# Moving the sums of a step's pairs behind the first bank of the second layer

## The chip, the cores and the metric

The kernel runs on one core of one Trainium2 chip. Its time is the device time of an execution in microseconds (us). Times of one kernel are compared through the median of several runs. Engines are named as in the profile: PE is TensorE (the matmuls), PEld its weight loads, DVE is VectorE, ACT is ScalarE, POOL is GpSimd, SP is SyncE, which issues DMA transfers.

## The reference

A layer of a graph network: 6250 nodes with 128 features (`x`), 100,000 edges (`src`, `dst`) sorted by destination, a hidden width of 256.

```python
msg_in = concatenate([x[src], x[dst]], axis=-1)
h = relu(msg_in @ Wm1 + bm1)
h = relu(h @ Wm2 + bm2)
messages = h @ Wm3 + bm3
agg = segment_sum(messages, dst) / clip(count, 1)[:, None]
upd = relu(concatenate([x, agg]) @ Wn1 + bn1) @ Wn2 + bn2
return layernorm(x + (x + upd))
```

All inputs and the output are 32-bit floats (indices are integers).

## The kernel before

**Tables.** A prelude of some 85 us multiplies `x` by the two halves of `Wm1`: `atab` holds the half for the source, in 32-bit floats, `btab` the half for the destination, split into bf16 terms. Both lie in DRAM. `Wm3` is linear and is applied to a node's mean, behind the segment sum.

**Steps.** The edges come in 196 groups of 512 and the main loop runs over 98 steps of two groups. Iteration p works on several steps at once, in this order in the text of the program (lines of the kernel before):

- `turned` (L770): TensorE turns the partial sums of step p-3, six transposes into two banks, and DVE adds them to the windows of `acc` (`pair_window`, L743; `add_up`, L779, from step 82 on). Called T below.
- `node_steps(p, 0)`: pieces of the node network for finished nodes, in some steps.
- `make_hot(p + 1)`: DVE makes the one-hot matrices of the next step (L640, L642).
- `first_layer` of step p: 32 transposes of the gathered rows (L666), 16 for each group (X0, X1), then the products of btab's rows with the one-hot matrices (L674, four for each group; L683, eight for each group, from step 59 = `B_PAIRED` on; P0, P1). Both add into the PSUM tile `ph`. Two relus on ACT (L692) write `h1`.
- `fetch` of step p+1: eight gathers of atab's rows on POOL (L607), four or eight loads of btab's rows issued by SP (L620), which wait for the last product that reads their buffer.
- `summed(p - 2)`: matmuls with one-hot weights that add up the messages of a destination, 16 instructions in tiles 128*32 (`pair_sums`, L734, up to step 81 = `PAIRED` - 1; `sums`, L724, behind). Called S. ACT copies the result to `part` (`part_of`, L752).
- `second_layer` of step p-1: h1 times Wm2 in four banks of eight matmul instructions (L711), A and B for group 0, C and D for group 1; after each bank DVE takes the maximum with a row that stands for relu and bias, into `h2s` (L714). Between B and C stands `node_steps(p, 1)`, whose matmuls are those of L811, L817 and L844.

**What sets the order.** The order on each engine is the program's own: TensorE, ACT, POOL, SP and DVE run under `tc.manual_schedule`, which keeps the instructions of an engine in the order in which they are written. Semaphores are put in from the buffers that are read and written.

**Buffers.** PSUM has four banks that go round (`bank`): T takes two, S one, A to D one each, so a plain step with paired sums takes seven, in the order T0 T1 S A B C D. `h2s` has one copy for each group: the sums read what the four maxima of the iteration before wrote, and the maxima of this iteration wait until the sums have read. `h1`, `part` and the gathered rows have two copies.

**Marks.** A gather keeps TensorE's pace by three waits (`MARKS`): the first gather of a fetch for a step's sums (`("sums", 0)`), the fifth for the first matmul of bank D (`("second", 12)`), the seventh for the first product (`("products", 0)`).

```python
MARKS = {("sums", 0): 0, ("second", 12): 4, ("products", 0): 6}
```

**Matmuls of 32-bit floats** in banks and sums are two instruction pairs each (a weight load and a matmul), which the profile counts one by one.

Of the kernel before, what the change touches and what calls it, by code (L numbers as in the profile page):

```python
# [14 lines left out]
ALU = mybir.AluOpType  # L15
# [5 lines left out]
P = 128  # L21
# [9 lines left out]
def kernel(  # L31
# [36 lines left out]
    nc = tc.nc  # L68
    N, D = x.shape
    E = src.shape[0]  # L70
    H = wm1.shape[1]
    HC = H // P
# [112 lines left out]
    with tc.tile_pool(name="prep", bufs=1) as prep, tc.tile_pool(  # L185
# [249 lines left out]
        def whole(steps):  # L435
            for _ in steps:
                pass
# [105 lines left out]
    with edge, tc.tile_pool(name="wk", bufs=2) as wk, tc.tile_pool(  # L543
# [28 lines left out]
        def follows(key, made):  # L572

            if not straight[0]:
                return
            for old in earlier.get(key, []):
                tc.declare_no_dep(made.ins, old.ins, reason="TensorE's work between the two waits for the first, "
                                  "and the second waits for that work")

        def keep(key, made):  # L580
            if straight[0]:
                earlier[key] = (earlier.get(key, []) + [made])[-4:]
# [7 lines left out]
        def pace(i, stage, n, matmul):  # L590
            if (stage, n) in MARKS:
                paces.setdefault(i, {})[MARKS[stage, n]] = matmul
# [65 lines left out]


        def first_layer(got, ohts, nts, step):  # L660
            for i, ((ag, _, _), nt) in enumerate(zip(got, nts)):
                for c in range(HC):
                    for j in range(GT):
                        for h in range(nt // 2):
                            half = slice(h * HP, (h + 1) * HP)
                            nc.tensor.matmul(ph[:, i, h, c, j * HP:(j + 1) * HP], ag[half, j, c * P:(c + 1) * P],  # L666
                                             ident[half, half], is_transpose=True, start=(c == 0 and j == 0),
                                             stop=False, skip_group_check=True)
            for i, ((_, bw, paired), nt) in enumerate(zip(got, nts)):
                for c in range(HC):  # L670
                    if paired:
                        for h in range(2):
                            half = slice(h * HP, (h + 1) * HP)
                            matmul = nc.tensor.matmul(ph[:, i, h, c, :], bw[half, 0, c * P:(c + 1) * P],  # L674
                                                      ohts[half, i, :], start=False, stop=True,
                                                      skip_group_check=True)
                            pace(step + 1, "products", (i * HC + c) * 2 + h, matmul)
                            last_product[step] = matmul
                        continue
                    for k in range(2):  # L680
                        for h in range(nt // 2):
                            half = slice(h * HP, (h + 1) * HP)
                            matmul = nc.tensor.matmul(ph[:, i, h, c, k * P:(k + 1) * P],  # L683
                                                      bw[half, k, c * P:(c + 1) * P],
                                                      ohts[half, i, k * P:(k + 1) * P], start=False, stop=True,
                                                      skip_group_check=True)
                            if k == 0:
                                pace(step + 1, "products", (i * HC + c) * 2 + h, matmul)
                            last_product[step] = matmul
            h1 = next_h1()  # L690
            if nts == [GT, GT]:
                made = [nc.scalar.activation(h1[:, :, c, :].rearrange("p i (h e) -> p i h e", h=2),  # L692
                                             ph[:, :, :, c, :], AF.Relu, bias=b1[:, c:c + 1]) for c in range(HC)]
                for one in made:
                    follows(("h1", step % 2), one)
                for one in made:
                    keep(("h1", step % 2), one)
                return h1
            for i in reversed(range(len(nts))):
                nh = nts[i] // 2  # L700
                for c in range(HC):
                    nc.scalar.activation(h1[:, i, c, :nh * 2 * P].rearrange("p (h e) -> p h e", h=nh),
                                         ph[:, i, :nh, c, :], AF.Relu, bias=b1[:, c:c + 1])
            return h1

        def second_layer(h1, h2, nt, step, before):
            for j0 in range(0, nt, 2):
                ph2 = bank()
                for j in range(j0, j0 + 2):
                    for c in range(HC):  # L710
                        matmul = nc.tensor.matmul(ph2[:, j - j0, :], h1[:, c, j * P:(j + 1) * P],  # L711
                                                  w2[:, c, :], start=(c == 0), stop=(c == HC - 1))
                        pace(step + 2, "second", before + j * HC + c, matmul)
                made = nc.vector.tensor_tensor(h2[:, j0:j0 + 2, :H], ph2, nb2.to_broadcast([P, 2, H]), op=ALU.max)  # L714
                follows("copied", made)
                keep("largest", made)

        def sums(groups):

# [258 lines left out]
        for i in range(NP + 7):  # L978
            if i == 8:
                late_loads()  # L980

                none = wk.tile([16, (NG * GE - E) // 16 + 1], I32, name="none", bufs=1)
                nc.vector.memset(none, NONE)
                nc.sync.dma_start(dpad[E - 16:].rearrange("(p e) -> p e", p=16), none)
                nc.sync.dma_start(dpad[:E].rearrange("(p e) -> p e", p=16), dst.rearrange("(p e) -> p e", p=16))
            if i < NP:
                c = 2 * i // CG + 1
                if 2 * i % CG == 0 and 1 < c < NG // CG:
                    chunks[c] = chunk(c)
                queues = [(nc.sync, ENG.SP), (nc.scalar, ENG.Activation) if i == 0 else (nc.sync, ENG.SP)]  # L990
                firsts = b_firsts(i, [eng for _, eng in queues])
                st[i] = dict(nts=NTS[2 * i:2 * i + 2])
            p = i - 1
            if p < 0:
                st[i]["got"] = fetch(i, [(srcT[:, 2 * i + k, :], firsts[k]) for k in range(2)], [q for q, _ in queues])
                continue
            if p == 0:
                make_hot(0)
            k = p - 3
            if 0 <= k < NP:  # L1000
                if k < NP - 2:
                    load_firsts(k)
                pt = turned(st[k]["part"], [GT] if k < PAIRED else st[k]["nts"])
                if k < PAIRED:
                    pair_window(pt, st.pop(k)["firsts"])
                else:
                    add_up(pt, st[k]["firsts"], st.pop(k)["nts"])
            node_steps(p, 0)
            if p in X_LATER:
                whole(x_part(X_LATER[p], bank, (nc.scalar, nc.scalar)))  # L1010
            if p + 1 < NP:
                make_hot(p + 1)
            if p == 0:
                clear(3)
            if p < NP:
                s = st[p]
                s["h1"] = first_layer(s.pop("got"), s.pop("ohts"), s["nts"], p)
            if i < NP:
                st[i]["got"] = fetch(i, [(srcT[:, 2 * i + k, :], firsts[k]) for k in range(2)], [q for q, _ in queues],
                                     paces.pop(i, {}))  # L1020
            if p == 0:
                whole(x_part(X_FIRST, bank, (nc.scalar, nc.vector)))
            if 0 <= p - 2 < NP:
                pgs, matmul = summed(p - 2)
                pace(p + 2, "sums", 0, matmul)
                st[p - 2]["part"] = part_of(pgs, [GT] if p - 2 < PAIRED else st[p - 2]["nts"])
            if 0 <= p - 1 < NP:
                s = st[p - 1]
                for j, nt in enumerate(s["nts"]):
                    if p == NP and j == 1:  # L1030
                        load_firsts(NP - 2)
                        load_firsts(NP - 1)
                    second_layer(s["h1"][:, j], h2s[j], nt, p, j * GT * HC)
                    if j == 0:
                        node_steps(p, 1)
            else:
                node_steps(p, 1)
            if p in (1, 2):
                clear(2)
        assert not st and not slots and not plan  # L1040
# [82 lines left out]
```

## Time and profile before

| | us |
|---|---|
| runs: 1331.02, 1341.98, 1339.16; median | 1339.16 |
| the profiled execution | 1348.45 |
| its span, from the first to the last instruction | 1346.7 |
| its granted TensorE clock, share of full speed | 0.976 |

The profile shows one execution. A row of a group reads: line, engine, operation, output<-input, tile, shape, count, then busy us and mean ns of one, then the idle time of the engine just in front of these instructions and what ended most of it. "issue" is a wait that the profile cannot put down to anything. A row of a timeline reads: start, busy us, engine, line, operation, count, and in brackets the idle time before it. A gap of a few tenths of a microsecond between weight loads of different tile shapes is a change of the array's tiling.

The engines that serve TensorE in the groups of the page:

```profile
L607 POOL DMA_INDIRECT rows<-atab,srcT x784 | 746.1, 952 | 485.2 <-issue 166.8
L714 DVE TENSOR_TENSOR h<-bank,nb 128x512 f32<-128x512 f32 x391 | 264.9, 690 | 600.8 <-PE bank L711 407.4
L692 ACT ACTIVATE h<-ph,b 128x1024 f32<-128x1024 f32 x194 | 205.6, 1110 | 789.2 <-remote 393.5
L666 PE MATMUL ph<-ident,rows 64*128 64x64 f32 x3128 | 134.6, 226 | 38.1 <-issue 36.6
```

### The profile page before, as it was taken

Reading aid. Unit: us, or ns where it says so; the run is one execution under the profiler, and the core shown is the slowest. Engines: PE = TensorE matmul, PEld = TensorE weight load, DVE = VectorE, ACT = ScalarE, POOL = GpSimd, SP = SyncE. Lnnn points to the kernel's source line nnn. Section 1 sums busy time; section 2 is a strip of 40 time slices with the busy share of each in tenths; the row PEclk is TensorE's granted clock in tenths of the full one; section 3 lists DMA queues with packets and bytes.
Section 4 is the critical chain, followed back from the end, with each engine's and each line's share of the span. In section 5 each row is a group of like instructions: output and inputs, shape, how many; then the busy total and the mean of one; then the engine's idle time right before and its main releaser. Section 6 shows DMA issues by size and latency. Waiting matters only on the chain.

```text
span 1346.7 us, 26320 instructions
## 1 busy us (share of the span) xinstructions
PE 1237.1 (92%) x10288; PEld 935.8 (69%) x10289; DVE 618.8 (46%) x1502; ACT 335.5 (25%) x500; POOL 793.6 (59%) x854
## 2 busy tenths in 40 slices
PE   8988998999999999999999998989988999999996
PEld 6746666776776667766766766767767677777784
DVE  6754333333333334443444443534445454555675
ACT  4741221122122112222221222221222212223232
POOL 6666665665666666666666665655655655556531
PEclk9999999999999999999999999999999899999998
DMA  7963443433433334334343444434444434344320
GB/s 224 336 207 105 124 116 99 114 106 101 112 108 112 101 107 115 106 108 129 108 110 113 123 114 118 134 111 125 131 115 120 123 111 137 107 118 122 108 58 24
DMA packets 113876, 163.66 MB, mean 122 GB/s; under 512 B 24730, under 2 KB 74592, under 8 KB 113728
## 3 DMA queue, kind: packets, MB, share of 16 engines
q0 software_dynamic: 38160, 103.75, 27.5%
q1 hardware_dynamic: 67292, 44.97, 10.8%
q10 hardware_dynamic: 8292, 13.18, 3.4%
q8 instruction: 82, 1.34, 0.4%
q14 instruction: 50, 0.41, 0.1%
HBM read 142.35 MB, written 19.86 MB: 120 GB/s over the span
## 4 chain that ended last, share of the span: by engine, by line
PE 89%; issue 6%; DVE 4%; DMA 0%; ACT 0%; POOL 0%; DVEq 0%; SPq 0%; ACTq 0%; POOLq 0%
PE bank L711 53%; PE bank L734 11%; PE ph L666 9%; PE bank L770 3%; PE ph L674 2%; PE pbt L315 2%; PE ph L683 2%; PE bank L844 2%; PE bank L811 1%; PE bank L817 1%; PE bank L724 1%; PE pxu L426 1%; DVE h L714 1%; DVE acc L779 0%; DVE span_i L267 0%
## 5 line engine op out<-in xcount | busy, mean ns | idle before, releaser
L607 POOL DMA_INDIRECT rows<-atab,srcT x784 | 746.1, 952 | 485.2 <-issue 166.8
L711 PE MATMUL bank<-w,h 128*128 128x256 f32 x3128 | 722.6, 386 | 8.0 <-DVE h L714 4.1
L711 PEld LDWEIGHTS bank<-w,h 128*128 128x128 f32 x3128 | 592.5, 192 | 139.3 <-issue 52.5
L714 DVE TENSOR_TENSOR h<-bank,nb 128x512 f32<-128x512 f32 x391 | 264.9, 690 | 600.8 <-PE bank L711 407.4
L692 ACT ACTIVATE h<-ph,b 128x1024 f32<-128x1024 f32 x194 | 205.6, 1110 | 789.2 <-remote 393.5
L666 PE MATMUL ph<-ident,rows 64*128 64x64 f32 x3128 | 134.6, 226 | 38.1 <-issue 36.6
L734 PE MATMUL bank<-h,oh 128*32 128x257 f32 x1312 | 155.5, 409 | 12.4 <-issue 1.3
L666 PEld LDWEIGHTS ph<-ident,rows 64*128 64x128 f32 x3128 | 117.2, 141 | 49.7 <-issue 46.5
L734 PEld LDWEIGHTS bank<-h,oh 128*32 128x32 f32 x1312 | 46.8, 112 | 93.8 <-issue 77.1
L743 DVE TENSOR_TENSOR acc<-acc,bank 128x96 f32 x328 | 83.5, 255 | 40.2 <-remote 18.4
L770 PEld LDWEIGHTS bank<-ident,part 64*128 64x128 f32 x681 | 31.1, 137 | 48.1 <-issue 27.6
L770 PE MATMUL bank<-ident,part 64*128 64x64 f32 x681 | 46.8, 237 | 12.6 <-DVE h L714 8.6
L315 PE MATMUL pbt<-w,xT 128*128 128x256 f32 x196 | 47.6, 388 | 5.9 <-DVE rest L340 3.0
L752 ACT COPY part<-bank 128x257 f32<-128x257 f32 x114 | 42.1, 375 | 24.4 <-PE bank L711 17.3
L315 PEld LDWEIGHTS pbt<-w,xT 128*128 128x128 f32 x196 | 36.5, 194 | 13.4 <-DVE rest L340 4.2
L674 PE MATMUL ph<-oht,rows 64*128 64x256 bf16 x472 | 40.1, 275 | 4.2 <-issue 4.2
L683 PE MATMUL ph<-oht,rows 64*128 64x128 bf16 x620 | 32.7, 225 | 10.7 <-issue 10.0
L642 DVE TENSOR_TENSOR oh<-iota_w,dloc 128x256 f32<-128x256 f32 x82 | 34.3, 418 | 0.0
L779 DVE TENSOR_TENSOR acc<-acc,bank 128x63 f32 x126 | 27.8, 221 | 13.3 <-remote 4.5
L683 PEld LDWEIGHTS <-rows 64*128 64x128 bf16 x620 | 23.2, 99 | 14.8 <-issue 14.7
L640 DVE TENSOR_SCALAR oht<-db,iota_p 128x512 bf16<-128x512 bf16 x98 | 31.8, 324 | 0.0
L674 PEld LDWEIGHTS <-rows 64*128 64x128 bf16 x472 | 24.4, 97 | 7.2 <-issue 6.3
(167 smaller groups left out, 613.0 us busy)
## 6 DMA issues: line engine op xcount, KB each, us to landing
rows<-btab SPq DMA_DIRECT2D x544, 32.0 KB
db<-reltab ACTq DMA_DIRECT2D x98, 128.0 KB
rows<-atab,srcT POOLq DMA_INDIRECT x784
btab<-acc SPq DMA_DIRECT2D x24, 384.0 KB
atab<-at SPq DMA_DIRECT2D x24, 256.0 KB
x_sb<-in_x_dram SPq DMA_DIRECT2D x5, 512.0 KB
xd<-in_x_dram SPq DMA_DIRECT2D x6, 256.0 KB
out_dram<-xd SPq DMA_DIRECT2D x6, 256.0 KB
```

The costliest lines, as they stand in the source:

```text
L315: nc.tensor.matmul(pbt[:, a, :], xT[:, (t0 + a) * P:(t0 + a + 1) * P], w1[:, k, :], start=True, stop=True)
L607: gather = nc.gpsimd.indirect_dma_start(out=ag[:, j, :], out_offset=None, in_=atab[:, :], in_offset=bass.IndirectOffsetOnAxis(ap=idx[:, j: ...
L666: nc.tensor.matmul(ph[:, i, h, c, j * HP:(j + 1) * HP], ag[half, j, c * P:(c + 1) * P], ident[half, half], is_transpose=True, start=(c == ...
L674: matmul = nc.tensor.matmul(ph[:, i, h, c, :], bw[half, 0, c * P:(c + 1) * P], ohts[half, i, :], start=False, stop=True, skip_group_check= ...
L683: matmul = nc.tensor.matmul(ph[:, i, h, c, k * P:(k + 1) * P], bw[half, k, c * P:(c + 1) * P], ohts[half, i, k * P:(k + 1) * P], start=Fal ...
L692: made = [nc.scalar.activation(h1[:, :, c, :].rearrange("p i (h e) -> p i h e", h=2), ph[:, :, :, c, :], AF.Relu, bias=b1[:, c:c + 1]) for ...
L711: matmul = nc.tensor.matmul(ph2[:, j - j0, :], h1[:, c, j * P:(j + 1) * P], w2[:, c, :], start=(c == 0), stop=(c == HC - 1))
L714: made = nc.vector.tensor_tensor(h2[:, j0:j0 + 2, :H], ph2, nb2.to_broadcast([P, 2, H]), op=ALU.max)
L734: matmul = nc.tensor.matmul(pg[(2 * i + q) * WN:(2 * i + q + 1) * WN, :H + 1], oh[:, 2 * q + k, :], h2[:, 2 * q + k, :], start=k == 0, sto ...
L743: made = nc.vector.tensor_add(window, window, pts[q // 2][:, 0, :, k:k + WN])
L752: copied.append(nc.scalar.copy(part[:nt * WN, i], pg[:nt * WN, :H + 1]))
L770: nc.tensor.matmul(pts[r][:, i, c, :], rows, ident[half, half], is_transpose=True, start=True, stop=True, skip_group_check=True)
```

## The change

It changes the order of TensorE's instructions in an iteration, and with it that of the others where they follow.

- `first_layer` calls the new `first_group` for one group after the other: X0 P0 X1 P1 in place of X0 X1 P0 P1. The relus follow both, in the new function `relus`.
- `second_layer` is split into `second_bank` (the eight matmuls) and `largest` (DVE's maximum). In an iteration the matmuls of bank A now come in front of the sums; the sums and ACT's copy follow, then the maximum of A, then bank B with its maximum, `node_steps(p, 1)`, and banks C and D as before. The banks go round in the order T0 T1 A S B C D.
- The part of the node network's first layer that iteration 0 makes (`x_part(X_FIRST)`) and the loads of window positions in iteration 98 (`load_firsts`) move by a few instructions.

```diff
         def first_layer(got, ohts, nts, step):
...
+            for i in range(len(nts)):
+                first_group(i, got, ohts, nts, step)
+            return relus(nts, step)
+
+        def first_group(i, got, ohts, nts, step):
+            (ag, bw, paired), nt = got[i], nts[i]
+            for c in range(HC):
+                for j in range(GT):
+                    for h in range(nt // 2):
+                        half = slice(h * HP, (h + 1) * HP)
+                        nc.tensor.matmul(ph[:, i, h, c, j * HP:(j + 1) * HP], ag[half, j, c * P:(c + 1) * P],
+                                         ident[half, half], is_transpose=True, start=(c == 0 and j == 0),
+                                         stop=False, skip_group_check=True)
+            for c in range(HC):
+                if paired:
+                    for h in range(2):
+                        half = slice(h * HP, (h + 1) * HP)
+                        matmul = nc.tensor.matmul(ph[:, i, h, c, :], bw[half, 0, c * P:(c + 1) * P],
+                                                  ohts[half, i, :], start=False, stop=True,
+                                                  skip_group_check=True)
+                        pace(step + 1, "products", (i * HC + c) * 2 + h, matmul)
+                        last_product[step] = matmul
+                    continue
...
         def second_layer(h1, h2, nt, step, before):
             for j0 in range(0, nt, 2):
...
+                largest(second_bank(h1, j0, step, before), h2, j0)
+
+        def second_bank(h1, j0, step, before):
+            ph2 = bank()
+            for j in range(j0, j0 + 2):
+                for c in range(HC):
+                    matmul = nc.tensor.matmul(ph2[:, j - j0, :], h1[:, c, j * P:(j + 1) * P],
+                                              w2[:, c, :], start=(c == 0), stop=(c == HC - 1))
+                    pace(step + 2, "second", before + j * HC + c, matmul)
+            return ph2
+
+        def largest(ph2, h2, j0):
+            made = nc.vector.tensor_tensor(h2[:, j0:j0 + 2, :H], ph2, nb2.to_broadcast([P, 2, H]), op=ALU.max)
+            follows("copied", made)
+            keep("largest", made)
...
+            ph2 = second_bank(was["h1"][:, 0], 0, p, 0) if was else None
             if 0 <= p - 2 < NP:
                 pgs, matmul = summed(p - 2)
                 pace(p + 2, "sums", 0, matmul)
                 st[p - 2]["part"] = part_of(pgs, [GT] if p - 2 < PAIRED else st[p - 2]["nts"])
...
+            if was:
+                largest(ph2, h2s[0], 0)
+                largest(second_bank(was["h1"][:, 0], 2, p, 0), h2s[0], 2)
+            if p == 0:
+                whole(x_part(X_FIRST, bank, (nc.scalar, nc.vector)))
+            if p == NP:
+                load_firsts(NP - 2)
+                load_firsts(NP - 1)
+            node_steps(p, 1)
+            if was:
+                second_layer(was["h1"][:, 1], h2s[1], was["nts"][1], p, GT * HC)
```

More of the change, by code (lines that the diff above doesn't have):

```diff
@@ L660, in first_layer @@
         def first_layer(got, ohts, nts, step):
[L661 to L676, printed above, removed]
-                            pace(step + 1, "products", (i * HC + c) * 2 + h, matmul)
[L678 to L689, printed above, removed]
@@ new lines, in first_layer @@
+            for i in range(len(nts)):
[20 more added lines that the diff above has]
+                    continue
+                for k in range(2):
+                    for h in range(nt // 2):
+                        half = slice(h * HP, (h + 1) * HP)
+                        matmul = nc.tensor.matmul(ph[:, i, h, c, k * P:(k + 1) * P],
+                                                  bw[half, k, c * P:(c + 1) * P],
+                                                  ohts[half, i, k * P:(k + 1) * P], start=False, stop=True,
+                                                  skip_group_check=True)
+                        if k == 0:
+                            pace(step + 1, "products", (i * HC + c) * 2 + h, matmul)
+                        last_product[step] = matmul
@@ L690, in first_layer, with relus @@
+        def relus(nts, step):
             h1 = next_h1()
@@ L707, in second_layer @@
             for j0 in range(0, nt, 2):
[L708 to L716, printed above, removed]
+                largest(second_bank(h1, j0, step, before), h2, j0)
[11 more added lines that the diff above has]
+            keep("largest", made)
         def sums(groups):
@@ L1014 @@
                 clear(3)
-            if p < NP:
-                s = st[p]
-                s["h1"] = first_layer(s.pop("got"), s.pop("ohts"), s["nts"], p)
+            now = st[p] if p < NP else None
+            was = st[p - 1] if 0 <= p - 1 < NP else None
+            if now:
+                now["h1"] = first_layer(now.pop("got"), now.pop("ohts"), now["nts"], p)
             if i < NP:
@@ L1020 @@
                                      paces.pop(i, {}))
-            if p == 0:
-                whole(x_part(X_FIRST, bank, (nc.scalar, nc.vector)))
+            ph2 = second_bank(was["h1"][:, 0], 0, p, 0) if was else None
             if 0 <= p - 2 < NP:
@@ L1026 @@
                 st[p - 2]["part"] = part_of(pgs, [GT] if p - 2 < PAIRED else st[p - 2]["nts"])
[L1027 to L1037, printed above, removed]
+            if was:
[9 more added lines that the diff above has]
+                second_layer(was["h1"][:, 1], h2s[1], was["nts"][1], p, GT * HC)
             if p in (1, 2):
```

## The prediction

> **What bounds the kernel now.** I read the page first: busy shares, the chain that ended last, the groups.
>
> ```profile
> span 1346.7 us, 26320 instructions
> PE 1237.1 (92%) x10288; PEld 935.8 (69%) x10289; DVE 618.8 (46%) x1502; ACT 335.5 (25%) x500; POOL 793.6 (59%) x854
> PE 89%; issue 6%; DVE 4%; DMA 0%; ACT 0%; POOL 0%; DVEq 0%; SPq 0%; ACTq 0%; POOLq 0%
> ...
> L711 PE MATMUL bank<-w,h 128*128 128x256 f32 x3128 | 722.6, 386 | 8.0 <-DVE h L714 4.1
> ...
> L734 PE MATMUL bank<-h,oh 128*32 128x257 f32 x1312 | 155.5, 409 | 12.4 <-issue 1.3
> ...
> L734 PEld LDWEIGHTS bank<-h,oh 128*32 128x32 f32 x1312 | 46.8, 112 | 93.8 <-issue 77.1
> ```
>
> TensorE (PE) carries 89% of the chain. The sums (L734) count 155.5 us busy, but the row of their weight loads has 93.8 us of idle time in front of them, 77.1 of it "issue", a wait that the profile cannot name. A busy PE is therefore partly a PE that stands still between two of the sums. The groups of the sums' line by stage say where, the timeline of the weight loads (start, busy time, count, idle before) how:
>
> ```profile
> 105.00:820.00 715.00, 124.44 (x928) 35.21 (x928) 0.99 0.40 111
> 820.00:1122.00 302.00, 29.99 (x368) 11.20 (x368) 0.96 0.44 122
> ...
> 736.24 0.65 PEld L666 LDWEIGHTS ph<-ident,rows 64*128 64x128 f32 x18 [0.62 <-issue]
> 736.78 0.40 PEld L674 LDWEIGHTS <-rows 64*128 64x128 bf16 x8
> 737.39 0.14 PEld L734 LDWEIGHTS bank<-h,oh 128*32 128x32 f32 x4 [0.21 <-issue]
> 737.92 0.16 PEld L734 LDWEIGHTS bank<-h,oh 128*32 128x32 f32 x3 [0.38 <-issue]
> 738.67 0.15 PEld L734 LDWEIGHTS bank<-h,oh 128*32 128x32 f32 x4 [0.60 <-issue]
> 739.41 0.19 PEld L734 LDWEIGHTS bank<-h,oh 128*32 128x32 f32 x5 [0.58 <-issue]
> 740.01 6.77 PEld L711 LDWEIGHTS bank<-w,h 128*128 128x128 f32 x32 [0.41 <-issue]
> 747.12 0.26 PEld L770 LDWEIGHTS bank<-ident,part 64*128 64x128 f32 x6 [0.33 <-issue]
> ```
>
> The first two rows are windows: length, then busy time and count of the sums' matmuls and of their loads. Up to 820 us, 928/16 = 58 steps have 124.44/58 = 2.15 us of sums each; after it 368/16 = 23 steps have 1.30. In the timeline the sums come four, three, four and five at a time with 0.38, 0.60 and 0.58 us between (1.56 us), and the transposes have one such pause, 0.62.
>
> What do they wait for? The sums read h2s, which DVE's maximum of banks C and D of the step before (L714) has to write. In the DVE timeline those two stand here:
>
> ```profile
> 736.29 1.29 DVE L714 TENSOR_TENSOR h<-bank,nb 128x512 f32<-128x512 f32 x2 [1.91 <-PE bank L770]
> ```
>
> They end at 737.58, and the third pair of sums' matmuls (the first that needs group 1) is loaded at 737.92, 0.34 us later. So the sums stand too close behind the maxima. But their end explains only the first pause, not those of 0.60 and 0.58 us after it, when everything they need is there.
>
> **Does the step get shorter where the sums don't wait?** Two places test it. One is a step whose turned part was held by a DVE operation; from TensorE's timeline:
>
> ```profile
> 711.01 0.27 PE L770 MATMUL bank<-ident,part 64*128 64x64 f32 x1
> 712.28 0.39 PE L770 MATMUL bank<-ident,part 64*128 64x64 f32 x5 [1.00 <-DVE xd L847]
> 712.45 1.22 PE L666 MATMUL ph<-ident,rows 64*128 64x64 f32 x32
> 713.45 0.66 PE L674 MATMUL ph<-oht,rows 64*128 64x256 bf16 x8
> 714.03 1.08 PE L734 MATMUL bank<-h,oh 128*32 128x257 f32 x16
> ```
>
> Here the sums take 1.08 us, without a pause: that is their price unhindered. The other is the stretch from step 59 on, where the products are 16 instructions. Its weight loads:
>
> ```profile
> 876.62 0.15 PEld L666 LDWEIGHTS ph<-ident,rows 64*128 64x128 f32 x2 [0.62 <-issue]
> 877.33 0.14 PEld L666 LDWEIGHTS ph<-ident,rows 64*128 64x128 f32 x1 [0.55 <-issue]
> 878.04 0.14 PEld L666 LDWEIGHTS ph<-ident,rows 64*128 64x128 f32 x1 [0.57 <-issue]
> 878.07 0.51 PEld L683 LDWEIGHTS <-rows 64*128 64x128 bf16 x16
> 878.69 0.59 PEld L734 LDWEIGHTS bank<-h,oh 128*32 128x32 f32 x16
> ```
>
> The sums run through, yet three pauses of the same size, 0.62 + 0.55 + 0.57 = 1.74 us, stand in the transposes, which wait for no maximum. And work added between banks B and C costs a plain step little; TensorE's and ACT's timelines:
>
> ```profile
> 768.11 1.03 PE L811 MATMUL bank<-acc,w 128*128 128x256 f32 x4
> 772.82 1.21 PE L666 MATMUL ph<-ident,rows 64*128 64x64 f32 x32
> 751.86 1.11 ACT L692 ACTIVATE h<-ph,b 128x1024 f32<-128x1024 f32 x1 [8.30 <-remote]
> 764.18 2.12 ACT L692 ACTIVATE h<-ph,b 128x1024 f32<-128x1024 f32 x2 [9.94 <-remote]
> 776.47 2.12 ACT L692 ACTIVATE h<-ph,b 128x1024 f32<-128x1024 f32 x2 [9.90 <-remote]
> ```
>
> From relu to relu the plain step takes 764.18 − 751.86 = 12.32 us and the one with four more matmuls 12.29: the pause in its transposes is gone instead (32 in one run of 1.21 us). So some 2 us of standing still belong to a step, and they move to wherever TensorE is quickest. What paces it the rows do not say.
>
> **The change part by part.** Instruction counts and tiles are the same; only the order differs. Before: turned part T, transposes X0 X1, products P0 P1, sums S, banks A B C D. After: T X0 P0 X1 P1 A S B C D.
>
> *First layer by group.* X and P are both 64*128 tiles, and X to P has no switch in the rows above (736.78 follows at once), so P0 before X1 costs nothing. The two relus still wait for the last product. Gather 6 waits for the first product, which comes by half the transposes (0.6 us) earlier; GpSimd has room on either side:
>
> ```profile
> 746.07 0.95 POOL L607 DMA_INDIRECT rows<-atab,srcT  x1 [0.30 <-issue]
> 748.76 0.95 POOL L607 DMA_INDIRECT rows<-atab,srcT  x1 [1.74 <-PE bank L770]
> ```
>
> Eight gathers at 0.95 + 0.30 make 10.0 of 12.3 us. Gather 0 waits for the sums, now one bank (about 1.8 us: 6.77 us of loads and the 0.33 after them are four) later. What of that comes late is taken out of the 1.74 us before the later gather that waits for bank D. Cost nothing; without that cover at most 0.1 us a step (1.8 less 1.74). SP's loads wait for the last product, as before.
>
> *Sums behind A.* The wait for max D gains 1.8 us, against a lateness of 0.34: it goes. The upper bound of the gain is all excess of the sums over 1.08 us: 58 × 1.07 + 23 × 0.22 = 67 us. Max A now has to wait until the sums have read h2s[0]; DVE has only max B behind it. Bank D takes A's bank and comes after S, B and C (1.08 + 3.6 us behind A), and max A takes 0.65 (half of the 1.29 above), so about 3 us remain. ACT's copy comes a bank later; its reader, the next turned part, is three banks away (5.4 us). A takes the bank that max C freed, half of the same row, so at 736.94: half a microsecond before the sums stood there at 737.39. These are hidden. If completions are seen late (the row of max C and D names the turned part, L770, as what released them), the reserve at bank A is the first to fail.
>
> *One more switch of tile shape.* Before, a step has P to S 0.21, S to bank 0.41, D to T 0.33: 0.95 us. After, P to A, A to S, S to B, D to T. A start-up row has P to a bank:
>
> ```profile
> 91.25 0.51 PEld L711 LDWEIGHTS bank<-w,h 128*128 128x128 f32 x3 [0.21 <-issue]
> ```
>
> No row has a bank followed by sums; I bound it by 0.21 and 0.41 from the switches above and take 0.31, as it resembles both. A step then has 1.26 us of switches, 0.31 more. A gain of a switch is excluded, since none goes without another coming. [...]
>
> *The sum.* Freed in a plain step: the pauses of 0.62 + 1.56 = 2.18 us. Come back, by the stretch from step 59: 1.74. Net −0.44, and 0.31 for the switch: −0.13 × 58 = −7.5 us. From step 59 the pauses already lie in the transposes, and the added switch is taken out of them: 0. Start-up, end and node work are unchanged in amount. The profiled execution took 1348.45 us (span 1346.7), 9.3 above the median of 1339.16, which I take as base: 1339.2 − 7.5 = 1331.7, said as 1332. Ends of this case: switch absorbed everywhere −25.5 (1314); paid in all, −7.5 + 40 × 0.31 = +5 (1344).
>
> **Rivals.** *The pauses are an echo of the wait for max D and go with it.* For it: the 0.34 us; the clean 1.08 us where max D was early. Against it: the pauses from step 59. It gives −67 + 98 × 0.31 = −37: 1302; with the switch covered, 1272.
>
> [...]
>
> *The sums still dribble behind A.* If the wait for max C at bank A replaces that for max D, TensorE starts A late by the same third of a microsecond, the sums follow four by four, and the time is 1339 give or take the switch. It is part of "no change".
>
> **How the numbers follow.** A measurement of this kernel can tell about 1% from no change, 13 us. No change that it can tell (the sum and the dribbling sums) 0.40; the echo, faster, 0.37; the drain, slower, 0.23. The sum at 1332 is the likeliest, its own range 1314 to 1344. Most of the echo lies from 1284 to 1325 and most of the drain below 1372, so 1284 to 1372 leaves some 0.15 out.
>
> **What would show it.** In the changed kernel the sums' matmuls should take about 1.1 us a step, with no idle time for max D. If I am right, "issue" pauses stand in the transposes or in the sums still, near 1.7 us a step, and relus follow each other every 12.2 us. If the echo holds, relus come every 11.5 us or less. [...] Wrong altogether: DVE waiting at max A while bank D waits for it, or gathers that land after the transposes want them.

## The result and the profile after

The changed kernel takes 1407.41 us (median of 4 runs, 1404.86 to 1408.74), the kernel before 1337.35 on the same chip (1331.02 to 1341.98): a ratio of 1.0525, 95% interval 1.0477 to 1.0573. It is slower, by about 70 us, and outside the range. The two profiled executions differ by 58.6 us in span (1405.3 against 1346.7).

The page of the changed kernel (L720 is the second layer, L671 the transposes, L746 the sums, L678 the products of the first 59 steps):

```profile
span 1405.3 us, 26325 instructions
PE 83%; issue 10%; DVE 3%; DMA 1%; POOL 1%; ACT 1%; SPq 0%; DVEq 0%; POOLq 0%; ACTq 0%
...
L720 PE MATMUL bank<-w,h 128*128 128x256 f32 x3128 | 791.3, 406 | 4.9 <-issue 3.7
L720 PEld LDWEIGHTS bank<-w,h 128*128 128x128 f32 x3128 | 612.9, 201 | 160.7 <-issue 67.3
...
L671 PE MATMUL ph<-ident,rows 64*128 64x64 f32 x3128 | 165.1, 227 | 90.1 <-issue 88.6
...
L746 PE MATMUL bank<-h,oh 128*32 128x257 f32 x1312 | 96.4, 404 | 2.0 <-issue 2.0
```

The reader is to see where time left and where it came in. The sums fell from 155.5 to 96.4 us busy: nearly all of their pauses are gone. The idle time in front of the transposes rose from 38.1 to 90.1 us. And the second layer, with the same instructions as before, rose from 722.6 to 791.3 us busy. That last row is the one to ask about: why do equal matmuls take longer?

Two windows of the main loop (length, busy PE and count, granted clock, DMA share, GB/s), first of the changed kernel, then of the kernel before:

```profile
105.00:820.00 715.00, 637.98 (x5155) 0.92 0.37 104
820.00:1122.00 302.00, 272.88 (x2433) 0.98 0.42 119
```

```profile
105.00:820.00 715.00, 670.09 (x5531) 0.99 0.40 111
820.00:1122.00 302.00, 273.43 (x2513) 0.96 0.44 122
```

In the stretch of plain steps the granted clock fell from 0.99 to 0.92. TensorE's timeline there (start, busy us, operation, count, idle before) shows how, and behind it four windows of the same stretch:

```profile
202.85 0.40 PE L782 MATMUL bank<-ident,part 64*128 64x64 f32 x6
...
204.89 0.29 PE L671 MATMUL ph<-ident,rows 64*128 64x64 f32 x2 [0.49 <-issue]
206.32 0.63 PE L678 MATMUL ph<-oht,rows 64*128 64x256 bf16 x4 [1.14 <-issue]
206.88 3.39 PE L720 MATMUL bank<-w,h 128*128 128x256 f32 x8
210.20 1.08 PE L746 MATMUL bank<-h,oh 128*32 128x257 f32 x16
211.21 5.45 PE L720 MATMUL bank<-w,h 128*128 128x256 f32 x24
...
220.53 3.39 PE L720 MATMUL bank<-w,h 128*128 128x256 f32 x8
```

```profile
199.44:202.85 3.41, 3.41 (x17) 1.00 0.64 171
202.85:206.27 3.42, 1.84 (x43) 1.00 0.40 114
206.27:209.68 3.41, 3.36 (x11) 0.51 0.23 65
209.68:213.09 3.41, 3.41 (x28) 0.99 0.18 54
```

The pauses now stand behind the transposes and in front of the second group's products (0.49 and 1.14 us), and the sums follow bank A without one (1.08 us). But bank A takes 3.39 us. In a step at full clock the same eight matmuls are one row of 1.99 us:

```profile
748.23 1.99 PE L720 MATMUL bank<-w,h 128*128 128x256 f32 x8
```

The windows, cut where the record of the clock changes, show when it happens: one of 3.41 us that holds the turned part, the transposes, the first group's products and the pauses, and no bank and no sums, is followed by one at half clock (0.51), and bank A lies in it. Bank A of the next step starts at 220.53, 13.65 us later, which is four times 3.41: the half clock lengthens the step to just the length at which the next step meets the windows in the same way. Of the 69 us by which the second layer's busy time rose, some 26 are an effect of the count: bank A now stands alone, and 1.99 + 5.45 us for one and three banks are 0.27 a step more than 7.17 for four in a row. The half clock makes up most of the rest. From step to step (relu to relu) the trace has runs of 13.6 to 13.8 us and others of 12.3 to 12.5.

Counted from the record of the clock, between 105 us and 60 us before the end, 40 windows are at half clock, 13 in the kernel before. The place matters: between 105 and 820 us there are 32 against 4, from 820 to 1122 us 4 against 7. The kernel before thus shows it by itself: it had 4 half-clock windows before step 59, where the rows quoted in the prediction have its pauses in the sums, and 7 in the next 23 steps, where they have them in the transposes. At the start of step 59 (809.6 us before, 858.5 after) the changed kernel was already 49 us behind, of 58.6 at the end.

The next table asks what a window held before the clock fell. It takes the windows at full clock between 105 and 1145 us and counts how much of each was taken up by matmuls other than transposes ("dense" below); a matmul counts from its start to the start of the next, but no longer than it took itself. "Halved next" are those with a half-clock window right behind them.

```
share of dense work     before: windows, halved next     after: windows, halved next
under 0.1                   4        4                      20       18
0.1 to 0.2                  6        2                       9        4
0.2 to 0.4                 12        2                      26       12
0.4 and more              270        4                     213        1
```

In the window shown in front of the half clock TensorE was not idle: it was busy for 1.84 of its 3.42 us.

### The profile page after: what moved, and what is told of

Read it like the earlier page. It is cut to its first block, busy times and chain, and to the rows that moved or that the text cites. A ratio compares the mean times of both kernels' runs of the same rounds, so it can differ in the third digit from the quotient of the medians.

```text
span 1405.3 us, 26325 instructions
## 1 busy us (share of the span) xinstructions
PE 1255.1 (89%) x10288; PEld 953.4 (68%) x10289; DVE 627.6 (45%) x1502; ACT 337.9 (24%) x500; POOL 791.9 (56%) x854
## 4 chain that ended last, share of the span: by engine, by line
PE 83%; issue 10%; DVE 3%; DMA 1%; POOL 1%; ACT 1%; SPq 0%; DVEq 0%; POOLq 0%; ACTq 0%
PE bank L720 54%; PE ph L671 9%; PE bank L746 6%; PE ph L678 2%; PE bank L782 2%; PE bank L856 2%; PE ph L687 2%; PE pbt L315 2%; PE bank L823 1%; PE bank L829 1%; PE bank L736 1%; POOL rows L607 1%; DVE acc L791 0%; DMA btab<-acc 0%; DVE rest L340 0%
## 5 line engine op out<-in xcount | busy, mean ns | idle before, releaser
L720 PE MATMUL bank<-w,h 128*128 128x256 f32 x3128 | 791.3, 406 | 4.9 <-issue 3.7
L720 PEld LDWEIGHTS bank<-w,h 128*128 128x128 f32 x3128 | 612.9, 201 | 160.7 <-issue 67.3
L726 DVE TENSOR_TENSOR h<-bank,nb 128x512 f32<-128x512 f32 x391 | 269.9, 692 | 639.6 <-PE bank L746 284.1
L671 PE MATMUL ph<-ident,rows 64*128 64x64 f32 x3128 | 165.1, 227 | 90.1 <-issue 88.6
L671 PEld LDWEIGHTS ph<-ident,rows 64*128 64x128 f32 x3128 | 134.7, 141 | 97.7 <-issue 95.1
L746 PE MATMUL bank<-h,oh 128*32 128x257 f32 x1312 | 96.4, 404 | 2.0 <-issue 2.0
L746 PEld LDWEIGHTS bank<-h,oh 128*32 128x32 f32 x1312 | 37.5, 115 | 52.5 <-issue 37.9
L678 PE MATMUL ph<-oht,rows 64*128 64x256 bf16 x472 | 51.8, 292 | 19.6 <-issue 18.6
L687 PE MATMUL ph<-oht,rows 64*128 64x128 bf16 x620 | 37.9, 222 | 12.7 <-issue 12.7
L678 PEld LDWEIGHTS <-rows 64*128 64x128 bf16 x472 | 20.6, 100 | 32.8 <-issue 30.3
L782 PE MATMUL bank<-ident,part 64*128 64x64 f32 x681 | 42.0, 235 | 0.1
```

Source lines behind the costliest of these rows:

```text
L746: matmul = nc.tensor.matmul(pg[(2 * i + q) * WN:(2 * i + q + 1) * WN, :H + 1], oh[:, 2 * q + k, :], h2[:, 2 * q + k, :], start=k == 0, sto ...
L782: nc.tensor.matmul(pts[r][:, i, c, :], rows, ident[half, half], is_transpose=True, start=True, stop=True, skip_group_check=True)
```

## The experiments

They ran on chips numbered 15, 7, 6 and 11. The kernel before takes 1149 to 1151 us on each of them, not 1337, with the same program. The first result has no chip number on record; that it came from another chip is inferred from its time. Below, "the first chip" means that one, and "a chip without pauses" one of the four.

The "drain theory" of the expectations is the prediction's chance called the drain: that each added switch of tile shape costs its gap between weight loads in time, 0.21 to 0.41 us by the prediction's rows, so 21 to 40 us for one in each of 98 steps.

**The sums alone.** The first layer as before, bank A in front of the sums; against the changed kernel (shortened, the conditions around each line left out):

```diff
             if now:
-                now["h1"] = first_layer(now.pop("got"), now.pop("ohts"), now["nts"], p)
+                transposes(0, got, nts)
+                transposes(1, got, nts)
+                products(0, got, ohts, nts, p)
+                products(1, got, ohts, nts, p)
+                now["h1"] = relus(nts, p)
```

> Only the sums move: T X0 X1 P0 P1 A S B C D, the first layer as before. Gate theory (TensorE's clock is halved for a window of 3.41 us after a window that held little but transposes and pauses; the change lets such a stretch, turned part, transposes and products, run on into bank A with no sums in it): the stretch is as long as in the changed kernel, so 1385 to 1410 us, 25 or more half-clock windows in the main loop, mean clock about 0.94. Theory that the first layer by group costs the time: about 1337 us and a clock near 0.976. Theory of the added drain at a switch of tile shape: 1360 to 1380 us with the clock of before.

Measured: 1167.41 us, ratio 1.0155 (1.0138 to 1.0172), no half-clock window in the main loop. The gate theory could not show itself, because the chip has no pauses. The loss of 17.7 us is 0.18 us a step, a little under the 0.21 at which the drain theory starts.

**The first layer alone.** X0 P0 X1 P1, then sums, then bank A.

> Only the first layer goes by group: T X0 P0 X1 P1 S A B C D. Gate theory: the sums still end the stretch of transposes, so 1330 to 1345 us, clock 0.97 to 0.98, pauses in the sums as before. Theory that the first layer by group costs the time: 1385 to 1410 us. Drain theory: 1337 us (no switch is added).

Measured: 1149.43 us, ratio 0.9998 (0.9988 to 1.0008). The first layer by group costs nothing, as predicted. Its weight loads show what a step is without pauses:

```profile
650.30 0.26 PEld L789 LDWEIGHTS bank<-ident,part 64*128 64x128 f32 x6 [0.33 <-issue]
650.48 0.58 PEld L675 LDWEIGHTS ph<-ident,rows 64*128 64x128 f32 x16
650.98 0.16 PEld L685 LDWEIGHTS <-rows 64*128 64x128 bf16 x4
651.15 0.62 PEld L675 LDWEIGHTS ph<-ident,rows 64*128 64x128 f32 x16
651.69 0.16 PEld L685 LDWEIGHTS <-rows 64*128 64x128 bf16 x4
652.06 0.59 PEld L753 LDWEIGHTS bank<-h,oh 128*32 128x32 f32 x16 [0.21 <-DVE acc L762]
653.06 3.32 PEld L727 LDWEIGHTS bank<-w,h 128*128 128x128 f32 x16 [0.41 <-issue]
```

Only the three switches of tile shape are left, 0.33, 0.21 and 0.41 us. The sums stand right behind the products and do not wait for max D, which ended at 651.10 us, 0.96 us before their first load:

```profile
650.41 0.69 DVE L733 TENSOR_TENSOR h<-bank,nb 128x512 f32<-128x512 f32 x1 [1.03 <-PE bank L727]
```

**Bank A between the groups**, T X0 P0 A X1 P1 S B C D, and **A there with B in front of the sums**, T X0 P0 A X1 P1 B S C D (the first of the two, shortened in the same way):

```diff
+                transposes(0, got, nts)
+                products(0, got, ohts, nts, p)
+                bank_a = second_bank(h1[:, 0], 0, p, 0)
+                transposes(1, got, nts)
+                products(1, got, ohts, nts, p)
```

> Bank A stands between the two groups of the first layer: T X0 P0 A X1 P1 S B C D. No stretch without dense matmuls is then longer than half of one of before. Gate theory: no half-clock windows beyond those of before (under 15 in the main loop), 1310 to 1340 us; below 1310 if the pauses go too. Drain theory: two switches of tile shape more than in the kernel before, so 1380 us or more, above the changed kernel if it holds alone. Theory that a step cannot be shorter than about 12.2 us whatever the order: 1325 to 1345 us.

> Bank A between the groups and bank B before the sums: T X0 P0 A X1 P1 B S C D. Gate theory: as the run before, 1310 to 1340 us, no half-clock windows beyond those of before. If short instructions pause because TensorE has run out of instructions issued ahead, each short stretch now stands behind a long one and the pauses shrink: below 1300 us. Drain theory: 1400 us or more. Theory of a step that cannot be shorter than 12.2 us: 1325 to 1345 us.

Measured: 1178.65 us, ratio 1.025 (1.0232 to 1.0267), and 1202.35 us, ratio 1.0455 (1.0437 to 1.0472). With one, two and three switches more than before, the sums alone and these two lose 17.7, 28.9 and 52.6 us against 1149.74: divided by 98 steps and by the switches, 0.18, 0.15 and 0.18 us for each. In plain steps, from relu to relu, it is 10.07, 10.21 and 10.42 us against 9.86 (394.23 − 384.37 in the run with the first layer alone):

```profile
384.37 2.12 ACT L705 ACTIVATE h<-ph,b 128x1024 f32<-128x1024 f32 x2 [7.49 <-PE ph L685]
394.23 2.12 ACT L705 ACTIVATE h<-ph,b 128x1024 f32<-128x1024 f32 x2 [7.47 <-PE ph L685]
```

So each added switch costs 0.15 to 0.18 us a step there. The drain theory has the sign right and the price, 0.21 to 0.41, somewhat too high; what TensorE does in such a gap no trace shows. A step that cannot be shorter than 12.2 us is excluded on these chips. The two other theories are about pauses and could not be tried here.

**The changed kernel on another chip**, with two of the kernels above:

> The changed kernel as it is, once more, beside the kernel before on the same chip. On a chip whose TensorE pauses (before near 1337 us): 1400 to 1412 us, 25 or more half-clock windows in the main loop. On a chip without pauses (before near 1150 us), where the sums alone cost 1.55%: switch theory 1165 to 1171 us, as the sums alone; half-clock windows none; gate theory without pauses gives no loss beyond that.

> Only the sums move, first layer as before. On a chip with pauses: gate theory 1385 to 1412 us, clock near 0.94; if the first layer by group is what brings the half-clock windows, 1337 to 1365 us. On a chip without pauses: 1167 us again.

> Bank A between the two groups of the first layer. On a chip with pauses: gate theory no half-clock windows beyond those of before, 1310 to 1365 us (two switches more than before are 29 us, as the chip without pauses showed); if the half-clock windows come from something else, 1400 us or more. On a chip without pauses: 1179 us again.

Measured: 1166.93 us, ratio 1.0153 (1.0131 to 1.0175), clock 0.991; 1166.74 us; 1178.29 us; before 1148.67. So the whole change costs 18 us on a chip without pauses, all of it the sums' move. The sums alone were measured twice more and the first layer alone once more, with these expectations:

> Only the sums move. On a chip with pauses (before near 1337 us): 1385 to 1412 us with 25 or more half-clock windows, if the place of the sums brings them; 1337 to 1365 us if the first layer by group does. On a chip without: 1167 us.

> Only the first layer goes by group. On a chip with pauses: 1330 to 1350 us, half-clock windows as before, if the place of the sums brings them; 1385 us or more if the first layer by group does. On a chip without: 1149 us.

> Only the sums move. On a chip with pauses (before near 1337 us): 1385 to 1412 us with 25 or more half-clock windows. On a chip without: 1167 us.

Measured: 1166.91, 1150.38 and 1167.96 us, on chips without pauses again. Which half of the change brings the half clock on the first chip could thus not be tried. What pauses do to the clock was tried by making pauses.

**One pause made by hand.** Four ACT copies on a spare tile start when TensorE reaches a point and TensorE's next matmul waits for the last; the result is untouched.

```diff
+        def hold(last):
+            for k in range(4):
+                copy = nc.scalar.copy(held, held)
+                if k == 0:
+                    after(copy, last)
+            return copy
```

It stands between the groups of the first layer in front of the sums, then in the order of the changed kernel, then (one copy, behind the relus) between the halves of the sums.

> A pause made by hand: the second group's transposes wait for four ACT copies behind the first group's (about 1.8 us of standing still a step), order T X0 P0 pause X1 P1 S A B C D. On a chip without pauses the kernel is near 1150 us, so the pause alone gives 1150 + 98 x 1.8 = 1326. Gate theory: the pause stands among transposes, so half-clock windows come whatever follows the products: 20 or more of them in the main loop, some 1.4 us each, 1355 to 1400 us. If it is the bank in front of the sums that brings them: none, 1310 to 1335 us.

> The same pause in the order of the changed kernel, T X0 P0 pause X1 P1 A S B C D. Gate theory: 20 or more half-clock windows, the run before plus the switch (18 us), 1370 to 1420 us. If pauses don't matter to the clock: 1326 + 18 = 1344 us and no half-clock windows.

> The same length of pause (about 1.8 us) between the two halves of the sums, T X0 P0 X1 P1 S pause S A B C D, as in the kernel before on a chip with pauses. Gate theory: the stretch of transposes ends with the first sums, so fewer than 5 half-clock windows and 1320 to 1345 us, well below the run with the pause in the transposes. If any pause of that length closes the gate: as that run.

Measured: 1453.42, 1466.44 and 1427.96 us, before 1150.75; clock 0.917, 0.924 and 0.921; 61, 59 and 60 half-clock windows in the main loop. The pause was longer than meant, 2.14 us in front of the loads in the first two and 2.47 in the third; the weight loads behind it in the first and in the third:

```profile
651.22 0.58 PEld L692 LDWEIGHTS ph<-ident,rows 64*128 64x128 f32 x16 [2.14 <-ACT held L672]
643.79 0.16 PEld L768 LDWEIGHTS bank<-h,oh 128*32 128x32 f32 x8 [2.47 <-ACT held L670]
```

So all three times came out longer than expected. A chip without pauses gets the half clock when it is made to pause like this, and runs of steps of 13.5 to 13.8 us appear in all three. In the first kernel the sums stand in front of the banks and the half clock comes all the same, so the bank in front of the sums is not needed for it. But the third was expected to have under 5 such windows. One pause of 2.47 us between the two halves of the sums came with 60 half-clock windows, one of 2.14 us in the transposes with 61, so "among the sums" alone did not protect.

**Four short pauses**, modelled on those of the first chip: one between the groups and three inside the sums, as in the kernel before; or all four in the second group's transposes, as in the changed kernel, with the sums first, and with the bank first.

```diff
+                        pause((2 * k + i) * 2 + q, (1, 3, 5), matmul)
```

> Four short pauses made by hand as the kernel before shows them on the chip with pauses: one between the groups' transposes, three inside the sums (after the second, fourth and sixth of eight). Order T X0 X1 P0 P1 S A B C D, relus behind the sums. About 0.5 us each, 2 us a step: 1150 + 98 x 2.0 = 1346 without half-clock windows. Theory that the clock falls by how little dense work a window of 3.41 us holds, so that sums between the pauses keep it up: under 12 half-clock windows in the main loop, 1330 to 1365 us. Theory that only the amount of pause counts: 40 or more half-clock windows, 1400 us or more.

> The same four pauses, all among the second group's transposes, as the changed kernel shows them; sums still in front of the banks: T X0 P0 X1 P1 S A B C D. Theory of dense work in a window: 25 or more half-clock windows, 35 us or more above the run with the pauses in the sums. Theory that only the amount counts: within 12 us of that run.

> The four pauses among the second group's transposes, now in the whole order of the changed kernel: T X0 P0 X1 P1 A S B C D. Theory (pauses among transposes bring half-clock windows, the bank in front of the sums only a switch of tile shape): 40 or more half-clock windows, the run with the sums in front (1489 us) plus 0 to 25 us, clock 0.91 to 0.93. If the bank in front of the sums brings half-clock windows of its own: 1530 us or more.

Measured: 1451.68, 1488.87 and 1502.66 us (before 1149.86 for the first two, 1149.16 for the third); clock 0.991, 0.916 and 0.923; 2, 64 and 58 half-clock windows. The weight loads of a step of the first, then of the second:

```profile
645.51 0.57 PEld L693 LDWEIGHTS ph<-ident,rows 64*128 64x128 f32 x16 [0.58 <-ACT held L672]
646.00 0.38 PEld L704 LDWEIGHTS <-rows 64*128 64x128 bf16 x8
646.59 0.14 PEld L772 LDWEIGHTS bank<-h,oh 128*32 128x32 f32 x4 [0.21 <-DVE acc L782]
647.67 0.14 PEld L772 LDWEIGHTS bank<-h,oh 128*32 128x32 f32 x4 [0.94 <-ACT held L672]
648.78 0.14 PEld L772 LDWEIGHTS bank<-h,oh 128*32 128x32 f32 x4 [0.96 <-ACT held L672]
649.86 0.14 PEld L772 LDWEIGHTS bank<-h,oh 128*32 128x32 f32 x4 [0.94 <-ACT held L672]
```

```profile
652.84 0.20 PEld L693 LDWEIGHTS ph<-ident,rows 64*128 64x128 f32 x4 [0.50 <-ACT held L672]
653.62 0.20 PEld L693 LDWEIGHTS ph<-ident,rows 64*128 64x128 f32 x4 [0.58 <-ACT held L672]
654.41 0.20 PEld L693 LDWEIGHTS ph<-ident,rows 64*128 64x128 f32 x4 [0.58 <-ACT held L672]
655.20 0.29 PEld L693 LDWEIGHTS ph<-ident,rows 64*128 64x128 f32 x4 [0.58 <-ACT held L672]
```

The pauses inside the sums came out longer than meant, so the first kernel missed its number (1330 to 1365): its weight loads stand still 0.58 + 0.94 + 0.96 + 0.94 = 3.42 us a step, those of the second 0.50 + 3 × 0.58 = 2.24. The 302 us that the first kernel lost need no other cause (98 × 3.42 would be 335). Yet the second is 37 us slower. With 1.2 us less of standing still it has 62 half-clock windows more. Counted as above, 45 of its 46 windows with under 0.2 of dense work were followed by a half-clock one; the first kernel had no such window, and one half-clock window followed any of its 304. The two also differ in the order of the first layer (X0 X1 P0 P1 against X0 P0 X1 P1), which costs nothing without pauses (ratio 0.9998); with pauses it was not tried by itself. The bank in front of the sums adds 14 us, near the 18 of the switch, and no half-clock windows of its own.

Dense work alone is not the rule, though. In the kernel with one long pause in the sums, 24 of 24 windows with 0.40 to 0.45 of it were followed by a half-clock one; in the kernel with three short pauses there, none of 34. The traces of eight kernels with half-clock windows and of the sums alone and the first layer alone sort better when the time of a transpose is counted at half:

```
share of dense work and half the transposes     windows, halved next
under 0.35                                         127      125
0.35 to 0.5                                        274      175
0.5 and more                                      2327        3
```

The best single limit, 0.42, has 50 of the 2728 windows on its wrong side; with transposes left out the best, 0.30, has 112. The weight of a half was fitted afterwards, and no run tests it.

## Why the prediction was wrong

- **The wait for max D.** "It goes": the sums of the changed kernel take 1.08 us. But that wait was not what paced TensorE, and it did not cause the first pause either. In the quoted step the load at 737.92 waits for no semaphore in the trace; the next load that does, for DVE's maxima, is the seventh, at 737.97, and it follows the sixth within 0.02 us.
- **The pauses move to the transposes.** Right, and most of the loss comes of it. The idle time in front of the transposes' matmuls grew by 52 us while the sums lost 59 us of busy time.
- **The step that failed** is the sum: "Come back, by the stretch from step 59: 1.74. Net −0.44". It priced a pause among transposes like a pause among sums, by its length, and put the clock at nothing. The clock fell as well, to 40 half-clock windows from 13; made by hand, four short pauses among the transposes came with 64 such windows, one there and three in the sums with 2. The quoted rows before already had the place (1.74 us in the transposes from step 59 on), and the granted clock there was 0.96 against 0.99 earlier: the row of windows that was quoted showed it, and I didn't ask why. 40 less 13 half-clock windows, at 3.39 − 1.99 = 1.40 us each for bank A, make 38 us, an estimate. That no rival held a fall of the clock is why the range missed.
- **The added switch.** Bounded by 0.21 and 0.41 us, taken as 0.31 and then as absorbed by the pauses from step 59 on. The gaps between weight loads did grow by about that: in the changed kernel on a chip without pauses they are 0.33, 0.21, 0.33 and 0.41 us, 1.28 in all against 0.95. But the time shows 0.18 us a step (18 us), just under the bound, and it is not absorbed where there are no pauses. With two and three added switches it was 0.15 and 0.18 us for each. 38 + 18 = 56 of the 58.6 us between the two profiled executions; up to step 59 the same sum gives 28 × 1.40 + 59 × 0.18 = 50, against the 49 read there. That the switch is paid in full on the first chip too is inferred from this sum, not shown by a run there.
- **"Some 2 us of standing still belong to a step."** They belong to the chip or its condition: four numbered chips run the same program in 1150 us, and a plain step there, with the first layer by group, takes 9.86 us without them.
- **The first layer by group, POOL, ACT's copy, max A and bank D.** Costed at nothing: the first has a ratio of 0.9998 (0.9988 to 1.0008) on a chip without pauses. Of the others the changed kernel shows one wait that counts: in the step at 1029 us the transposes wait twice for gathers, 0.72 and 0.44 us.
- **The rivals.** The echo falls with the pauses' place. The drain is right that an added switch costs time, 0.18 us a step; that TensorE is drained at a switch no run shows, only the gap between weight loads and the time. Alone the switch would have made 1355 on the first chip (1337 + 18). Most of the loss, 38 of 58.6 us by the estimate above, came from the half clock, which none of them named.

Open stays what makes TensorE pause on the first chip. Its traces show it only as "issue", and no other run showed such pauses. Loading of instructions is an unlikely reason: the larger of the queues that the profile names "instruction" made 82 transfers in the kernel before and 82 in the kernel with the first layer alone, of 1.04 and 0.99 us (medians), while the pauses come three or four to a step.

## What to carry to other kernels

Where the granted clock of a stage is below 1, ask how little dense work the windows in front of the slow matmuls held: in the changed kernel, with windows of 3.41 us, the half clock followed 18 of the 20 with under 0.1 of it. Then try an order in which dense matmuls stand between the transposes and waits, and short single waits: here four short pauses came with 2 half-clock windows where sums stood between them and with 64 in one stretch of transposes, and one pause of 2.47 us inside the sums came with 60. Price a change of order by its switches of tile shape (here 0.15 to 0.18 us each) and count them around the whole step; the loop before had the least possible, three for three shapes. And before explaining a wait that the profile cannot name, see whether the same program shows it on another chip.

## What the runs showed that was not expected

One program took 1337 us in the first measurement and 1148 to 1153 us on four numbered chips: 16%, most of it from pauses of some 0.6 us that no dependence in the profile explains. And in the changed kernel the step locked to the clock's windows: with a half-clock window on a bank, a step of 12.35 us became one of 13.65, four windows of 3.41, and the next one met the windows in the same place; this held for one run of fifteen steps and one of seven.
